# Layer 0's transposed input: read at a stride of eight floats from the tile where it lands, in place of a ScalarE copy that lays it out contiguously

## The chip, the cores and the metric

The kernel runs on one NeuronCore of a Trainium2 chip. The core has TensorE (matmul, PE in the profile, with its weight loads in a row of their own, PEld), VectorE (DVE), ScalarE (ACT), GpSimd (POOL) and SyncE (SP), which here issues every DMA. The metric is the time of one execution on the device in microseconds, and the figure given for a kernel is the median of its runs.

## The reference

Two layers of masked attention over 128 independent graphs of 128 tokens with 512 features, in float32. `x` is [128, 128, 512] and `adj` is [128, 128, 128] of booleans.

```python
# layer 0: 4 heads of 64; layer 1: 8 heads of 64, with its own layer norm ahead of the projections
def _L0_gnn_ref(x, adjacency_mask, Wq, Wk, Wv, Wo, bo):
    q, k, v = split_heads(x @ Wq), split_heads(x @ Wk), split_heads(x @ Wv)
    sim = jnp.einsum('bhid,bhjd->bhij', q, k) * scale
    sim = jnp.where(adjacency_mask[:, None, :, :], sim, neg)
    out = jnp.einsum('bhij,bhjd->bhid', softmax(sim), v)
    return merge_heads(out) @ Wo + bo

x = _layernorm(x + _L0_gnn_ref(x, adj, ...))
x = _layernorm(x + _L1_gnn_ref(x, adj, ...))   # adj or the diagonal; gamma, beta; 8 heads
```

Only one thing of it matters here: layer 0's three projections multiply `x` by weights over the feature axis. TensorE sums over the partition axis, so `x`, which arrives with tokens on the partitions, has to be turned so that features lie on the partitions and tokens along them.

## The kernel before, in words

The 128 graphs are taken in 64 groups of two (`G = 2`). A group passes through a software pipeline whose order is written out by hand: `opening`, then `step(s)` for s = 2 to 63, then `closing` and `last`. One step works on several groups at once: layer 0's projections of group s, layer 0's scores of group s - 1, its output product of group s - 2, and layer 1's stages of the groups before. Every engine runs its instructions strictly in the order in which the step emits them.

All large products are done as seven smaller ones (Strassen's scheme): a product of 2 by 2 blocks is made of seven block products of sums and differences of the blocks. "2 by 2" means here the two graphs of the group by the two halves of the features (`KH = 2` chunks of 128 features each). GpSimd makes the four sums of the input (`sums`, which calls `halves_sums`, L292). `product_0` (L362 to L399) issues layer 0's seven products; products 1, 2 and 4 take a block of the input itself, products 5, 6, 3 and 7 take one of the sums. Each product has six matmuls: query, key and value (t = 0, 1, 2) by two chunks. For query and key the input block is the moving operand, for value it is the stationary one (L384, L385). `out_product` (L402 to L427) does the same for the output projections: after each of its products VectorE adds the accumulator into the residual rows (L427), and the accumulators' banks, `a`, `c` and `f`, are used again by later products of the same seven.

The turning of `x` for groups 3 to 63 goes through memory, in five stages:

1. `turn(0, g)`: VectorE transposes blocks of 32 by 32, one instruction per graph (L219), into the tile `turned`.
2. `put`: one DMA of 512 KB writes `turned` to a scratch tensor in HBM (L204).
3. `arrive(0, g)`: four DMAs of 128 KB (L210) bring it back with the blocks on the right partitions, into `raw`, in which a partition holds 4 token blocks by 2 graphs by 4 chunks by 32 tokens. Layer 1 uses the same tile for its own input.
4. `in_order(g)`: at the start of the next step ScalarE copies `raw` into `xT0`, where the 128 tokens of a graph and chunk are contiguous; one instruction per graph (L246).
5. `sums(0, g)` on GpSimd and `product_0` on TensorE read `xT0`.

The order around these stages in a step is:

```python
        made = scores(s)
        load(s + 1)
        if s > 2:
            in_order(s)
            sums(0, s)
        masked(made, s, 0, 1, 2)
        attend(s)
```

`product_0(s, 1)` comes after `attend`; `turn(0, s + 1)` stands late in the step, among layer 1's value products and its output product (`v(s - 3, 7, 3)`, `turn(0, s + 1)`, `v(s - 3, 4)`, `out_product(1, s - 4, 6, 5)`); `arrive(0, s + 1)` is near the step's end. Groups 0, 1 and 2 are turned by TensorE itself (`transposed`), and the result is copied out of PSUM by ScalarE for one graph and by VectorE for the other (L236).

Of the kernel before, what the change touches and what calls it, by code (L numbers as in the profile page):

```python
# [10 lines left out]
F32 = mybir.dt.float32  # L11
U8 = mybir.dt.uint8
AF = mybir.ActivationFunctionType
ALU = mybir.AluOpType
# [3 lines left out]
P = 128  # L18
D = 64
G = 2  # L20
# [7 lines left out]
def kernel(ctx: ExitStack, tc: tile.TileContext, x, adj, wq, wk, wv, wo, bo,  # L28
                            gamma, beta, w_qkv, w_out, b_out, out):
    nc = tc.nc  # L30
    B, N, E = x.shape
    KC = E // P
    NG = B // G
    T = G * N
# [4 lines left out]
    one = ctx.enter_context(tc.tile_pool(name="one", bufs=1))  # L39
# [10 lines left out]
    def mm_tile(name):  # L50
        return ps_mm.tile([P, 512], F32, tag="mm", name=name)
# [102 lines left out]
    KH = KC // 2  # L154
# [42 lines left out]
    RATIO, XT, QK, V, QKV = {}, {}, {}, {}, {}  # L197
# [9 lines left out]
    def fetch(dst, scr):  # L207
        src = scr.rearrange("(a r) q x -> r q a x", r=32)
        for q in range(4):
            nc.sync.dma_start(dst[32 * q:32 * q + 32], src[:, q])  # L210

    SCR, RAW = {}, {}

    def turn(l, g):
        if not 0 <= g < NG:
            return
        t = one.tile([P, 4, G * KC * 32], F32, tag="turned", bufs=2, name=f"turned{l}_{g}")
        for b in range(G):
            nc.vector.transpose(t.rearrange("p a (b c i) -> p a b c i", b=G, c=KC)[:, :, b],  # L219
                                R[g][:, b].rearrange("p (c a i) -> p a c i", a=4, i=32))  # L220
        SCR[l] = put(t, f"scr{l}_{g}")

    def arrive(l, g):
        if not 0 <= g < NG:
            return
        RAW[l] = one.tile([P, 4, G, KC, 32], F32, tag="raw", name=f"raw{l}_{g}")
        fetch(RAW[l].rearrange("p a b c i -> p a (b c i)"), SCR[l])

    def transposed(g):

        xT = XT[0, g] = one.tile([P, KC, T], F32, tag="xT0", name=f"xT0_{g}")
        for b in range(G):
            pt = mm_tile(f"xt{g}_{b}")
            for c in range(KC):
                nc.tensor.transpose(pt[:, c * N:(c + 1) * N], R[g][:, b, c * P:(c + 1) * P], ident)
            (nc.scalar.copy, nc.vector.tensor_copy)[b](xT[:, :, b * N:(b + 1) * N],  # L236
                                                       pt.rearrange("p (c n) -> p c n", c=KC))
        sums(0, g)

    def in_order(g):  # L240

        if not 0 <= g < NG:
            return
        xT = XT[0, g] = one.tile([P, KC, T], F32, tag="xT0", name=f"xT0_{g}")
        for b in range(G):
            nc.scalar.copy(xT[:, :, b * N:(b + 1) * N].rearrange("p c (a j) -> p a c j", a=4),  # L246
                           RAW[0][:, :, b])

    def finish(g, half):

# [29 lines left out]
    def sums(l, g):  # L280
        if not 0 <= g < NG:
            return
        xs = XS[l, g] = one.tile([P, 4, KH, N], F32, tag=f"xs{l}", name=f"xs{l}_{g}")
        halves_sums(xs, XT[l, g].rearrange("p (h c) (b n) -> p b h c n", h=2, b=2))

    def halves_sums(xs, a):
        s1, s2, s3, s4 = (xs[:, i] for i in range(4))
        for o, a0, a1, op in ((s1, a[:, 1, 0], a[:, 1, 1], ALU.add),
                              (s2, s1, a[:, 0, 0], ALU.subtract),
                              (s4, a[:, 0, 1], s2, ALU.subtract),  # L290
                              (s3, a[:, 0, 0], a[:, 1, 0], ALU.subtract)):
            nc.gpsimd.tensor_tensor(o, a0, a1, op=op)  # L292


    XS, ACC, EV = {}, {}, {}
# [66 lines left out]
    def product_0(g, *which):  # L362

        if not 0 <= g < NG:
            return
        xT = XT[0, g].rearrange("p (h c) (b n) -> p b h c n", h=2, b=2)
        xs = XS[0, g]
        for i in which:
            left = {1: xT[:, 0, 0], 2: xT[:, 0, 1], 3: xs[:, 3], 4: xT[:, 1, 1], 5: xs[:, 0],
                    6: xs[:, 1], 7: xs[:, 2]}[i]  # L370
            right = {1: w0[:, :KH, 0], 2: w0[:, KH:, 0], 3: w0[:, KH:, 1], 4: ws0[:, 2],
                     5: w0[:, :KH, 1], 6: ws0[:, 0], 7: ws0[:, 1]}[i]
            bank, first = INTO[i]
            if i == 1:

                QKV[g] = two.tile([P, G, 2, 3, P], F32, tag="qkv0", name=f"qkv0_{g}")
            if first and bank == "c":
                ACC[0, bank] = mm_tile(f"c0_{g}")
            elif first:
                ACC[0, bank] = ps_st.tile([P, 512], F32, tag=f"{bank}0", name=f"{bank}0_{g}")  # L380
            acc = ACC[0, bank]
            todo = [(t, c) for t in range(3) for c in range(KH)]
            for n, (t, c) in enumerate(todo):
                lhsT, rhs = (right[:, c, t], left[:, c]) if t < 2 else (left[:, c], right[:, c, t])  # L384
                nc.tensor.matmul(acc[:, t * P:(t + 1) * P], lhsT, rhs, start=first and n == 0,  # L385
                                 stop=n == len(todo) - 1, skip_group_check=True)
            src = acc[:, :3 * P]

            def whole(b, h):
                return QKV[g][:, b, h].rearrange("p t n -> p (t n)")  # L390

            if i in (1, 5, 6):
                EV[0, i] = one.tile([P, 512], F32, tag=f"e{i}", name=f"e0_{i}_{g}")[:, :3 * P]
                nc.scalar.copy(EV[0, i], src)
            elif i == 4:
                nc.scalar.copy(whole(1, 0), src)
            else:
                b, h, e = {2: (0, 0, 1), 3: (0, 1, 6), 7: (1, 1, 5)}[i]
                nc.vector.tensor_add(whole(b, h), src, EV[0, e])  # L399
# [31 lines left out]
    SM, TOTAL, NMAX, PT, AT, SO = {}, {}, {}, {}, {}, {}  # L431
# [150 lines left out]
    def out_sums(l, g):  # L582
        if not 0 <= g < NG:
            return
        K = HEADS[l] // 2
        so = SO[l, g] = one.tile([P, 4, K // 2, N], F32, tag=("so", "xs0")[l], name=f"so{l}_{g}")
        halves_sums(so, AT[l, g].rearrange("p b (h c) n -> p b h c n", h=2))

    def addend(l, g):

# [145 lines left out]
    def step(s):  # L736

        direct = s in (2, 3)
        made = scores(s)
        load(s + 1)  # L740
        if s > 2:
            in_order(s)
            sums(0, s)
        masked(made, s, 0, 1, 2)
        attend(s)
        maxima(s, 0)
        if s > 3:
            maxima(s, 1)
        out_sums(0, s - 2)
        exps(s, 0, 0)  # L750
        product_0(s, 1)
        exps(s, 0, 1)
        out_product(0, s - 2, 1, 2, 5)
        if s == 3:
            maxima(s, 1)
        maxima(s, 2)
        product_0(s, 2)
        normalised(s, 0)
        out_product(0, s - 2, 6, 3)
        exps(s, 1, 0)  # L760
        stats(0, s - 2, 0)
        product_0(s, 6)
        exps(s, 1, 1)
        out_product(0, s - 2, 7)
        product_0(s, 5)
        out_product(0, s - 2, 4)
        stats(0, s - 2, 1)
        exps(s, 2, 0)
        product_0(s, 7)
        exps(s, 2, 1)  # L770
        normalised(s, 1)
        product_0(s, 3)
        blocks(s, 0)
        flush()
        product_0(s, 4)
        if direct:
            prepare(len(setup) - (s == 2))
        else:
            turn(1, s - 2)
        out_sums(1, s - 4)  # L780
        v(s - 3, 1, 2)
        out_product(1, s - 4, 1)
        if not direct:
            arrive(1, s - 2)
        blocks(s, 1)
        probs_arrive(s, 0)
        v(s - 3, 6, 5)
        out_product(1, s - 4, 2)
        normalised(s, 2)
        v(s - 3, 7, 3)  # L790
        turn(0, s + 1)
        v(s - 3, 4)
        flush(latest)
        cleared(s + 1, 0, 1)
        if direct:
            finish_direct(s - 2)
        else:
            finish(s - 2, 0)
        if s == 2:
            weight_sums(w1qk, wsqk, 1)  # L800
            prepare(1)
        out_product(1, s - 4, 6, 5)
        if not direct:
            finish(s - 2, 1)
        out_product(1, s - 4, 7, 3, 4)
        blocks(s, 2)
        probs_arrive(s, 1)
        stats(1, s - 4, 0)
        stats(1, s - 4, 1)
        arrive(0, s + 1)  # L810
        probs_arrive(s, 2)
        cleared(s + 1, 2)
        addend(0, s - 1)
        with_self(s - 2)
        qk(s - 2, 1, 2, 6)
        flush()
        qk(s - 2, 5)
        addend(1, s - 3)
        qk(s - 2, 7, 3, 4)
        if s == 2:  # L820
            weight_sums(w1v, wsv, 0, 1)
        if s == 3:
            weight_sums_out(1)
# [130 lines left out]
```

## Time and profile before

| | |
|---|---|
| median of three runs (lowest, highest) | 2784.31 us (2784.19, 2784.57) |
| profiled execution, from its first to its last instruction (span) | 2782.9 us |
| PE busy, of the span | 2768.0 us, 99% |
| PEld busy | 2609.2 us, 94% |
| DVE busy | 1789.9 us, 64% |
| ACT busy | 1502.5 us, 54% |
| POOL busy | 1752.2 us, 63% |
| mean granted TensorE clock | 0.999 of full |
| one step of the steady state | 42.84 us |
| L246, ScalarE's copy `xT<-raw` | 122 of 621 ns on average, 69.6 us busy |
| L219, VectorE's transpose `turned<-r` (both layers) | 242 of 678 ns |
| L292, GpSimd's sums of the inputs (both layers) | 512 of 732 to 740 ns |

The profile is of one execution of its own. For that execution the page gives the span, and no other time; the three timed runs lie 1.3 to 1.7 us above that span, which is what surrounds the instructions. A busy share says how long an engine had an instruction in work, not whether that work was on the path that sets the end; "PE" and "PEld" overlap each other by design. In the timeline a row that merges several instructions gives the start of the first and the length from there to the end of the last, so consecutive rows of PE overlap by the time that a matmul needs to drain, and the pace is read from start to start. Names are written as output <- inputs; for PE the first input is the moving operand and the second the stationary one.

### The profile page before, as it was taken

To read this page: it belongs to the slowest core of one execution; us is meant where nothing else is said; L and a number is where in the kernel's file an instruction comes from. 1 tells how busy PE (TensorE), PEld (TensorE's weight loads), DVE (VectorE), ACT (ScalarE), POOL (GpSimd) and SP (SyncE) were. 2 spreads that over 40 slices of the span, in tenths; PEclk is the share of its full clock that TensorE was granted. 3 is DMA by queue.
4 is the path that set the end of the run, shared out by engine and by line. 5 is a ranking of instruction groups with operands and counts; after the bars stand their busy time and mean duration, and the time that the engine had idled before them with its cause. 6 is when DMAs were issued, how large, how long until landed. Compare 5 with 4: busy or idle time off the path is not lost.

```text
span 2782.9 us, 63227 instructions
## 1 busy us (share of the span) xinstructions
PE 2768.0 (99%) x23317; PEld 2609.2 (94%) x23317; DVE 1789.9 (64%) x3303; ACT 1502.5 (54%) x4811; POOL 1752.2 (63%) x2311
## 2 busy tenths in 40 slices
PE   9999999999999999999999999999999999999998
PEld 8999999999999999999999999999999999999997
DVE  5766666666666666666666666666666666666665
ACT  3554555645555556455555564555555645555554
POOL 5656566666565666666656666666566666665664
PEclk9999999999999999999999999999999999999999
DMA  5345455464564554644545546455454464554532
GB/s 170 115 138 173 128 158 154 130 175 138 138 171 127 161 153 129 177 138 138 169 129 161 153 127 177 139 138 166 128 165 148 128 179 136 145 165 126 160 107 69
DMA packets 281812, 405.24 MB, mean 146 GB/s; under 512 B 44696, under 2 KB 206496, under 8 KB 281504
## 3 DMA queue, kind: packets, MB, share of 16 engines
q1 hardware_dynamic: 281504, 401.20, 49.5%
q8 instruction: 185, 3.03, 0.5%
q14 instruction: 123, 1.01, 0.1%
HBM read 205.00 MB, written 196.08 MB: 144 GB/s over the span
## 4 chain that ended last, share of the span: by engine, by line
PE 96%; issue 1%; POOL 1%; DVE 1%; DMA 1%; ACT 0%; SPq 0%; POOLq 0%; ACTq 0%; DVEq 0%
PE qka L329 16%; PE a L385 12%; PE oa L423 12%; PE qkf L329 8%; PE va L329 8%; PE av L575 6%; PE f L385 6%; PE of L423 6%; PE qkc L329 4%; PE vf L329 4%; PE c L385 3%; PE oc L423 3%; PE sc L456 2%; PE sc L462 2%; PE vc L329 2%; PE sc_a L462 2%
## 5 line engine op out<-in xcount | busy, mean ns | idle before, releaser
L514 POOL TENSOR_TENSOR sm<-sm,rec 128x1024 f32<-128x1024 f32 x192 | 364.1, 1896 | 383.4 <-DVE rec L513 383.1
L505 ACT ACTIVATE sm<-sm,nmax 128x128 f32<-128x128 f32 x1536 | 595.2, 393 | 4.9 <-DVE nmax L496 4.3
L596 POOL TENSOR_TENSOR r<-r,bias 128x1024 f32<-128x1024 f32 x128 | 302.0, 2359 | 63.5 <-ACT r L595 63.5
L427 DVE TENSOR_TENSOR r<-oa,r 128x256 f32<-128x256 f32 x508 | 212.3, 418 | 199.7 <-PE oa L423 191.6
L292 POOL TENSOR_TENSOR xs<-xT 128x256 f32<-128x256 f32 x256 | 189.4, 740 | 211.0 <-ACT xT L246 164.9
L505 ACT ACTIVATION_READ_ACCUMULATOR sm<-sm,nmax 128x1 f32 x1536 | 294.8, 192 | 0.0
L355 ACT COPY eqk<-qka 128x512 f32<-128x512 f32 x128 | 75.0, 586 | 349.3 <-PE qka L329 349.3
L490 DVE COPY_PREDICATED sm<-m,sc 128x512 f32<-128x512 uint8 x256 | 173.0, 729 | 134.9 <-PE sc L456 134.9
L329 PE MATMUL qka<-xs,wsqk 128*128 128x128 f32 x2048 | 249.7, 275 | 0.3 <-POOL xs L292 0.3
L329 PE MATMUL qkf<-xs,w 128*128 128x128 f32 x2048 | 249.8, 275 | 0.0
L529 DVE STREAM_TRANSPOSE turnedp<-sm 128x1024 f32<-128x1024 f32 x189 | 234.0, 1238 | 17.1 <-DMA scrp<-turnedp 11.8
L329 PEld LDWEIGHTS qka<-xs,wsqk 128*128 128x128 f32 x2048 | 239.0, 192 | 0.5 <-POOL xs L292 0.5
L329 PEld LDWEIGHTS qkf<-xs,w 128*128 128x128 f32 x2048 | 239.0, 192 | 0.0
L360 DVE TENSOR_TENSOR qk<-qka,eqk 128x512 f32<-128x512 f32 x64 | 44.3, 692 | 291.1 <-PE qka L329 286.1
L496 DVE TENSOR_REDUCE nmax<-sm 128x8 f32<-128x1024 f32 x192 | 226.4, 1206 | 0.1
L423 PE MATMUL oa<-wso,so 128*128 128x256 f32 x760 | 206.0, 380 | 0.7 <-DVE r L427 0.7
L423 PE MATMUL of<-wo,so 128*128 128x256 f32 x760 | 205.6, 379 | 0.7 <-POOL so L292 0.7
L615 POOL TENSOR_SCALAR ve<-mv 128x2 f32<-128x2 f32 x191 | 40.8, 214 | 261.3 <-DVE mv L608 255.1
L641 ACT ACTIVATE r<-r,shift,root 128x512 f32<-128x512 f32 x254 | 192.4, 807 | 8.7 <-POOL shift L630 4.7
L476 POOL MEMSET sm<- 128x1024 f32 x192 | 178.8, 951 | 0.0
L607 DVE BATCH_NORM_STATS2 st<-r 128x6 f32<-128x512 f32 x254 | 171.7, 676 | 4.4
L423 PEld LDWEIGHTS of<-wo,so 128*128 128x128 f32 x760 | 144.1, 190 | 20.9 <-POOL so L292 1.1
(159 smaller groups left out, 6799.9 us busy)
## 6 DMA issues: line engine op xcount, KB each, us to landing
scrp<-turnedp SPq DMA_DIRECT2D x189, 512.0 KB, 3.0
pT<-scrp SPq DMA_DIRECT2D x756, 128.0 KB, 4.1
scr<-turned SPq DMA_DIRECT2D x121, 512.0 KB, 4.4
raw<-scr SPq DMA_DIRECT2D x484, 128.0 KB, 3.6
r<-in_x_dram SPq DMA_DIRECT2D x63, 512.0 KB, 3.9
out_dram<-r SPq DMA_DIRECT2D x63, 512.0 KB, 5.0
m<-in_adj_dram SPq DMA_DIRECT2D x64, 32.0 KB, 3.7
raw_r<-in_L_gnn_w_qkv_dram SPq DMA_DIRECT2D x8, 256.0 KB, 4.2
```

Of the source, the lines that this page charges most:

```text
L292: nc.gpsimd.tensor_tensor(o, a0, a1, op=op)
L329: nc.tensor.matmul(o, lhsT, rhs, start=first and n == 0, stop=n == len(todo) - 1, skip_group_check=True)
L385: nc.tensor.matmul(acc[:, t * P:(t + 1) * P], lhsT, rhs, start=first and n == 0, stop=n == len(todo) - 1, skip_group_check=True)
L423: nc.tensor.matmul(acc, left[:, c], right[:, c], start=first and c == 0, stop=c == hk - 1, skip_group_check=True)
L427: nc.vector.tensor_add(part, acc, part)
L476: nc.gpsimd.memset(sm, NEG1 if part else NEG0)
L496: nc.vector.tensor_reduce(NMAX[part], SM[part], AX.X, ALU.max, negate=True)
L505: nc.scalar.activation(sm[:, i, k, :], sm[:, i, k, :], AF.Exp, bias=nmax[:, i, k:k + 1], accum_out=total[:, i, k:k + 1])
L514: nc.gpsimd.tensor_tensor(SM[part], SM[part], rec[:, :, :, None].to_broadcast([P, 2, K1, N]), op=ALU.mult)
L529: nc.vector.transpose(t.rearrange("p q (h r) -> p q h r", r=32), SM.pop(part).rearrange("p i k (q r) -> p q (i k) r", r=32))
L596: nc.gpsimd.tensor_tensor(R[g], R[g], (bias0, bias1)[l][:, None, :].to_broadcast([P, G, E]), op=ALU.add)
L641: nc.scalar.activation(R[g][:, b], R[g][:, b], AF.Identity, bias=shift[:, b:b + 1], scale=root[:, b:b + 1])
```

## The change

`in_order` and the tile `xT0` go. `turn(0, g)` makes VectorE write its transposes in another order, so that a partition of `raw` holds 128 tokens by 2 graphs by 4 chunks: the token is the slowest index, and the 128 tokens of one graph and chunk lie eight floats (32 bytes) apart. The DMAs move the same bytes in the same pieces. GpSimd's sums and the products 1, 2 and 4 of `product_0` read this tile directly, at the stride. Layers 0 and 1 now have raw tiles of their own, `raw0` and `raw1`; with `xT0` gone the memory used is the same. For groups 0 to 2, `transposed` copies out of PSUM into the same layout. `halves_sums` is rewritten to take its blocks from a table; for layer 1 and the output products it does what it did.

```diff
     def turn(l, g):
...
         for b in range(G):
-            nc.vector.transpose(t.rearrange("p a (b c i) -> p a b c i", b=G, c=KC)[:, :, b],
+            to = (t.rearrange("p a (b c i) -> p a b c i", b=G, c=KC)[:, :, b] if l else
+                  t.rearrange("p a (i b c) -> p b a c i", b=G, c=KC)[:, b])
+            nc.vector.transpose(to,
                                 R[g][:, b].rearrange("p (c a i) -> p a c i", a=4, i=32))
         SCR[l] = put(t, f"scr{l}_{g}")
 
     def arrive(l, g):
         if not 0 <= g < NG:
             return
-        RAW[l] = one.tile([P, 4, G, KC, 32], F32, tag="raw", name=f"raw{l}_{g}")
-        fetch(RAW[l].rearrange("p a b c i -> p a (b c i)"), SCR[l])
+        if l == 0:
+            RAW[0] = one.tile([P, N, G, KC], F32, tag="raw0", name=f"raw0_{g}")
+            fetch(RAW[0].rearrange("p (a i) b c -> p a (i b c)", a=4), SCR[0])
+        else:
+            RAW[1] = one.tile([P, 4, G, KC, 32], F32, tag="raw1", name=f"raw1_{g}")
+            fetch(RAW[1].rearrange("p a b c i -> p a (b c i)"), SCR[1])
 
     def transposed(g):
 
-        xT = XT[0, g] = one.tile([P, KC, T], F32, tag="xT0", name=f"xT0_{g}")
+        raw = RAW[0] = one.tile([P, N, G, KC], F32, tag="raw0", name=f"raw0_{g}")
...
-            (nc.scalar.copy, nc.vector.tensor_copy)[b](xT[:, :, b * N:(b + 1) * N],
+            (nc.scalar.copy, nc.vector.tensor_copy)[b](raw[:, :, b].rearrange("p n c -> p c n"),
                                                        pt.rearrange("p (c n) -> p c n", c=KC))
         sums(0, g)
-
-    def in_order(g):
-
-        if not 0 <= g < NG:
-            return
-        xT = XT[0, g] = one.tile([P, KC, T], F32, tag="xT0", name=f"xT0_{g}")
-        for b in range(G):
-            nc.scalar.copy(xT[:, :, b * N:(b + 1) * N].rearrange("p c (a j) -> p a c j", a=4),
-                           RAW[0][:, :, b])
...
     def sums(l, g):
...
-        halves_sums(xs, XT[l, g].rearrange("p (h c) (b n) -> p b h c n", h=2, b=2))
+        if l == 0:
+            halves_sums(*quarters(xs, RAW[0].rearrange("p n b (h c) -> p b h c n", h=2)))
+        else:
+            halves_sums(*quarters(xs, XT[l, g].rearrange("p (h c) (b n) -> p b h c n", h=2, b=2)))
+
+    def quarters(xs, a):
+        return [xs[:, i] for i in range(4)], {(b, h): a[:, b, h] for b in range(2) for h in range(2)}
...
     def product_0(g, *which):
...
-        xT = XT[0, g].rearrange("p (h c) (b n) -> p b h c n", h=2, b=2)
-        xs = XS[0, g]
+        xs, raw = XS[0, g], RAW[0]
         for i in which:
-            left = {1: xT[:, 0, 0], 2: xT[:, 0, 1], 3: xs[:, 3], 4: xT[:, 1, 1], 5: xs[:, 0],
-                    6: xs[:, 1], 7: xs[:, 2]}[i]
+            piece = {1: (0, 0), 2: (0, 1), 4: (1, 1)}.get(i)
+
+            def left(c):
+                return (raw[:, :, piece[0], piece[1] * KH + c] if piece else
+                        xs[:, {3: 3, 5: 0, 6: 1, 7: 2}[i], c])
+
...
-                lhsT, rhs = (right[:, c, t], left[:, c]) if t < 2 else (left[:, c], right[:, c, t])
+                lhsT, rhs = (right[:, c, t], left(c)) if t < 2 else (left(c), right[:, c, t])
...
     def step(s):
...
         if s > 2:
-            in_order(s)
             sums(0, s)
```

More of the change, by code (lines that the diff above doesn't have):

```diff
@@ L283, in sums @@
         xs = XS[l, g] = one.tile([P, 4, KH, N], F32, tag=f"xs{l}", name=f"xs{l}_{g}")
-        halves_sums(xs, XT[l, g].rearrange("p (h c) (b n) -> p b h c n", h=2, b=2))
-    def halves_sums(xs, a):
[L287 to L291, printed above, removed]
+        if l == 0:
[4 more added lines that the diff above has]
+        return [xs[:, i] for i in range(4)], {(b, h): a[:, b, h] for b in range(2) for h in range(2)}
+    def halves_sums(xs, a):
+        s1, s2, s3, s4 = xs
+        for o, a0, a1, op in ((s1, a[1, 0], a[1, 1], ALU.add),
+                              (s2, s1, a[0, 0], ALU.subtract),
+                              (s4, a[0, 1], s2, ALU.subtract),
+                              (s3, a[0, 0], a[1, 0], ALU.subtract)):
             nc.gpsimd.tensor_tensor(o, a0, a1, op=op)
@@ L586, in out_sums @@
         so = SO[l, g] = one.tile([P, 4, K // 2, N], F32, tag=("so", "xs0")[l], name=f"so{l}_{g}")
-        halves_sums(so, AT[l, g].rearrange("p b (h c) n -> p b h c n", h=2))
+        halves_sums(*quarters(so, AT[l, g].rearrange("p b (h c) n -> p b h c n", h=2)))
     def addend(l, g):
```

## The prediction

> **What bounds the kernel now.** I read four views, in this order. First the page's busy times and its chain of waits, then one whole step of the steady state by engine, for 1352.51 to 1395.35 us:
>
> ```profile
> PE 2768.0 (99%) x23317; PEld 2609.2 (94%) x23317; DVE 1789.9 (64%) x3303; ACT 1502.5 (54%) x4811; POOL 1752.2 (63%) x2311
> PE 96%; issue 1%; POOL 1%; DVE 1%; DMA 1%; ACT 0%; SPq 0%; POOLq 0%; ACTq 0%; DVEq 0%
> 1352.51:1395.35 42.84, 42.84 (x365) 40.47 (x366) 27.68 (x52) 23.38 (x75) 27.30 (x37) 1.00 0.49 149
> ```
>
> The reader is to see that TensorE has no gap: 42.84 us of matmul in a 42.84 us step, and a chain that is 96% PE. ScalarE, from which the change takes work, is busy 23.4 us of 42.8 and has 0% of the chain. So the edit is worth what it does to PE, and what it makes late for PE.
>
> Third, the timeline, PE alone, where layer 0's products begin:
>
> ```profile
> 1355.21 1.16 PE L385 MATMUL a<-xT,w 128*128 128x128 f32 x8
> 1356.21 0.61 PE L385 MATMUL a<-w,xT 128*128 128x128 f32 x4
> ...
> 1357.95 1.05 PE L385 MATMUL c<-xT,w 128*128 128x128 f32 x8
> 1358.85 0.61 PE L385 MATMUL c<-w,xT 128*128 128x128 f32 x4
> 1359.29 0.60 PE L423 MATMUL oa<-wso,so 128*128 128x256 f32 x2
> ```
>
> Columns: start, length, then output <- moving operand, stationary operand. One matmul of the loop leaves two records, so a product's six are twelve passes: eight with xT moving (query and key), four with xT stationary (value). Start to start, 8 passes take 1358.85 - 1357.95 = 0.90 us and 4 take 0.44, so a pass costs 111.5 ns for 128 columns, 0.87 ns a column. The weight loads run beside the matmuls at the same pace, one per pass (40.47 us of 42.84).
>
> Fourth, who waits for the ScalarE copy that goes, and what ScalarE does after it (waits; timeline, ACT):
>
> ```profile
> POOL xs L292 <- ACT xT L246: 164.9, 61, 5.5
> 1350.15 1.14 ACT L246 COPY xT<-raw 128x512 f32<-128x512 f32 x2
> 1353.59 0.59 ACT L578 COPY aT<-av 128x512 f32<-128x512 f32 x1 [2.29 <-PE av L575]
> ```
>
> GpSimd alone waits for it, in time in which it had nothing else; behind it ScalarE sits idle 2.29 us until PE delivers. Nothing that PE waits for comes earlier when the copy goes.
>
> [...]
>
> **The change part by part.**
>
> *Removed:* L246, 122 copies of 621 ns, 1.24 us a step on ScalarE. Off the path, as shown: worth 0. A gain would need a PE wait that ends earlier, and I see none.
>
> *PE reads layer 0's input at the stride.* Products 1, 2 and 4 are touched; 3, 5, 6 and 7 read the sums, which stay contiguous. [...] I take half rate[...]: 128 columns cost 128 x 0.83 = 107 ns more (0.83: 215 ns for 256 columns in L423, four passes in 0.86 us). [...] Both operands have the stride in some passes: eight stream it; four load it as weights, and a load that takes 214 ns no longer fits under a 111.5 ns matmul. The first of the four is loaded under the last slow stream, so 8 + 3 = 11 slow passes: 11 x 107 = 1.18 us a product, 3.53 us a step, and for 64 groups **+226 us**. Nothing covers it, PE being full.
>
> *VectorE writes the transposes at the stride* (L219 for layer 0, two a step). Where they stand (timelines, DVE and PE):
>
> ```profile
> 1332.33 1.29 DVE L219 STREAM_TRANSPOSE turned<-r 128x512 f32<-128x512 f32 x2
> 1333.72 0.42 DVE L427 TENSOR_TENSOR r<-oa,r 128x256 f32<-128x256 f32 x1
> 1334.58 0.42 DVE L427 TENSOR_TENSOR r<-of,r 128x256 f32<-128x256 f32 x1 [0.44 <-PE of L423]
> ...
> 1332.65 1.03 PE L423 MATMUL oa<-wso,so 128*128 128x256 f32 x4
> 1333.52 1.03 PE L423 MATMUL of<-wo,so 128*128 128x256 f32 x4
> 1334.38 1.03 PE L423 MATMUL oa<-wso,so 128*128 128x256 f32 x4
> ```
>
> Behind them in VectorE's queue is the evacuation of layer 1's output product 6, and PE may not write that bank again (product 7, its weights loaded from 1334.26) before VectorE has read it (done 1334.14). Slack: 0.10 us between the transposes' end (1333.62) and the evacuation, 0.12 after it, together 0.22. [...] A pair is then 1.1 us late, PE waits 0.88 us in each of the 59 steps that have this product (s = 4 to 62): **+52 us** (0 to 75). It can't be caught up, since PE has no idle time later.
>
> *GpSimd's four sums* (735 ns; 128 more columns cost 272 ns) read the stride. [...] They can start at 1348.72, when the bias addition ends, instead of 1351.37: 2.65 us earlier. PE's first need behind them is layer 0's output sum s1, ready at 1354.84, its product's weights loaded at 1357.31: another 2.47 us. So 0, up to 5.1 us a step (2.7 times the duration); past that product 5 is late.
>
> *Queues.* SP's DMAs stay in number, size and order (one put of 512 KB, four fetches of 128 KB). The put waits for VectorE and slips 1.1 us: issued at 1334.22, landed 4.4 us later, so 2.9 us before the first fetch at 1341.53: covered, and with it the fetches of probabilities queued behind. The fetch now waits until PE and GpSimd have read the tile instead of ScalarE: product 4 is over at 1367.7, the next fetch comes at 1384.4, 16.7 us later. POOL issues no DMA. Two raw tiles instead of one only loosen.
>
> *The opening's three direct groups:* ScalarE and VectorE write at the stride once for each[...]; only the first stands in PE's way: +1 us (0 to 4).
>
> **Sum:** 226 + 52 + 1 = 279 us. Against the profiled execution's span of 2782.9 that is 3062; the runs' median lies 1.4 us above that span, so **3063 us** (+10%).
>
> **The rivals.**
>
> 1. *Only VectorE pays* (0.20). [...] 2784 + 53 = 2837 (2800 to 2865).
> 2. *One of TensorE's operands pays* (0.12): weights alone 4 x 107 x 192 products = 82 us, streams alone 164; with the transposes 2919 or 3001 (2870 to 3010).
> 3. *More than half rate* (0.09): [...] (above 3120).
> 4. *Not slower* (0.06; and 0.01 for over 0.2% faster). One place decides, PE at L385: if its ports hold 0.87 ns a column, and the transposes stay under 0.11 us longer each, both fit into today's slack and nothing is left but a copy that cost nothing: 2784 (2779 to 2789). For it, GpSimd's and the queues' cover[...]. That the change does not do what it says I rule out: the copy's instruction is gone and the operands' steps are written in the diff.
>
> **How the numbers follow.** My forecast, both TensorE operands and the transposes, has 0.52, with its own range of 2995 to 3120 (PE 190 to 250, VectorE 20 to 77). The time is that of this case. The 8-in-10 range runs over cases 1, 2 and this, 2795 to 3120: 0.84 less their tails. A measurement can tell 0.2%, 5.6 us. Slower: 0.52 + 0.20 + 0.12 + 0.09 = 0.93; within: 0.06; faster: 0.01.
>
> **What would show it.** In the changed profile: matmuls of L385 that stream the raw tile start 215 to 220 ns apart, as do those that load it, and products of the sums stay at 111.5; if the former stay at 111.5 too, the main step is wrong. L219 for layer 0 takes 1.0 to 1.4 us, for layer 1 still 0.67, and PE gains a wait for VectorE's L427 of some 0.9 us a step; without it the 52 us fall. ScalarE's busy time falls by about 70 us. GpSimd's sums from the raw tile near 1 us, ahead of need; a PE wait for xs or so would break that step.

## The result, and the profile after

| | before | changed |
|---|---|---|
| median | 2784.44 us (2784.19 to 2785.08) | **3061.32 us** (3060.71 to 3061.97) |
| ratio to before, 95% interval | | **1.0994** (1.0979 to 1.1010) |
| span of the profiled execution | 2782.9 us | 3059.3 us |
| one step of the steady state | 42.84 us | 47.27 us |

Before's median is of four executions here, one more than above. The kernel is 277 us, 10%, slower. A step grew by 4.43 us. The page of the changed kernel, busy times and chain of waits; then one of its steps by engine:

```profile
PE 3032.3 (99%) x23317; PEld 2830.4 (93%) x23317; DVE 1824.8 (60%) x3303; ACT 1455.4 (48%) x4689; POOL 1790.0 (59%) x2311
PE 93%; DVE 5%; issue 1%; POOL 0%; ACT 0%; DMA 0%; SPq 0%; POOLq 0%; ACTq 0%; DVEq 0%
```

```profile
976.37:1023.64 47.27, 47.04 (x363) 43.94 (x363) 28.20 (x52) 22.68 (x73) 27.87 (x36) 1.00 0.47 135
```

PE issues the same 23317 matmuls, is still busy for 99% of the span at full clock (1.00 in this step), and yet needs 264 us more for them. That is the sign to look for: not a wait, but the same instructions taking longer. The one new thing on the chain is VectorE, 5%. The timeline of PE, from product 2 of layer 0 on (bank `c`), shows which instructions grew:

```profile
980.35 2.02 PE L391 MATMUL c<-raw,w 128*128 128x128 f32 x8
982.19 0.99 PE L391 MATMUL c<-w,raw 128*128 128x128 f32 x4
983.02 0.60 PE L429 MATMUL oa<-wso,so 128*128 128x256 f32 x2
...
983.88 1.05 PE L391 MATMUL a<-xs,ws 128*128 128x128 f32 x8
984.78 0.61 PE L391 MATMUL a<-ws,xs 128*128 128x128 f32 x4
985.22 0.60 PE L429 MATMUL oa<-wso,so 128*128 128x256 f32 x2
```

Start to start, eight passes that stream the raw tile take 1.84 us, 230 ns each; four that load it as weights take 0.83 us, 207 ns each; the product of the sums beside them still takes 0.90 and 0.44 us, 112 and 110 ns a pass. Product 2 grew from 1.34 to 2.67 us.

Next the place where the transposes stand. An evacuation is VectorE's addition of a product's accumulator into the residual rows (L433, L427 before); it frees the accumulator's bank. The timeline of VectorE, then that of PE, and last what PE waited for (waits, PE alone):

```profile
1000.22 2.04 DVE L221 STREAM_TRANSPOSE turned<-r 128x512 f32<-128x512 f32 x2
1002.10 0.41 DVE L433 TENSOR_TENSOR r<-oa,r 128x256 f32<-128x256 f32 x1
1002.47 0.42 DVE L433 TENSOR_TENSOR r<-of,r 128x256 f32<-128x256 f32 x1
```

```profile
1000.54 1.03 PE L429 MATMUL oa<-wso,so 128*128 128x256 f32 x4
1001.40 1.03 PE L429 MATMUL of<-wo,so 128*128 128x256 f32 x4
1002.66 1.10 PE L429 MATMUL oa<-wso,so 128*128 128x256 f32 x4 [0.23 <-DVE r L433]
1003.59 1.03 PE L429 MATMUL of<-wo,so 128*128 128x256 f32 x4
```

```profile
PE oa L429 <- DVE r L433: 13.4, 59, 0.3
```

The row of before that follows the three of PE in the prediction:

```profile
1335.24 1.03 PE L423 MATMUL of<-wo,so 128*128 128x256 f32 x4
```

The four PE rows of each kernel are products 6, 5, 7 and 3 of the output product. Two transposes take 2.04 us instead of 1.29. The evacuation of product 6 starts at 1002.10 without a wait, 1.56 us after product 6 itself (1000.54); before it was 1.07 us (1332.65 to 1333.72), so it is 0.49 us late. Product 7 starts 1.26 us after product 5, where it was 0.86, and product 3 another 0.93 us later, where it was 0.86: from product 5 to product 3 it is 2.19 us against 1.72, and PE loses 0.47 us. The waits view books less, 0.23, because the row of product 5 runs to 1002.43, 0.17 us beyond its pace of 0.86, and covers the first part of the gap. It happens 59 times, once in each step that has this product: 59 x 0.47 = 28 us.

GpSimd, the one that had waited for the copy (timeline, POOL):

```profile
969.76 0.66 POOL L295 TENSOR_TENSOR xs<-raw 128x256 f32<-128x256 f32 x1
...
972.24 1.14 POOL L295 TENSOR_TENSOR xs<-raw 128x256 f32<-128x256 f32 x1
```

The sums are done at 973.4, ten microseconds before the first product that reads them (983.88).

### The profile page after: what moved, and what is told of

It reads as the page before. It is cut to its first block, busy times and chain, and to the rows that moved or that the text cites. A ratio compares the mean times of both kernels' runs of the same rounds, so it can differ in the third digit from the quotient of the medians.

```text
span 3059.3 us, 63048 instructions
## 1 busy us (share of the span) xinstructions
PE 3032.3 (99%) x23317; PEld 2830.4 (93%) x23317; DVE 1824.8 (60%) x3303; ACT 1455.4 (48%) x4689; POOL 1790.0 (59%) x2311
## 4 chain that ended last, share of the span: by engine, by line
PE 93%; DVE 5%; issue 1%; POOL 0%; ACT 0%; DMA 0%; SPq 0%; POOLq 0%; ACTq 0%; DVEq 0%
PE a L391 17%; PE qka L332 15%; PE oa L429 9%; PE qkf L332 7%; PE av L581 6%; PE c L391 6%; PE f L391 6%; PE va L332 6%; DVE turned L221 4%; PE qkc L332 4%; PE of L429 4%; PE vf L332 4%; PE oc L429 3%; PE sc L462 2%; PE sc L468 2%; PE vc L332 2%
## 5 line engine op out<-in xcount | busy, mean ns | idle before, releaser
L433 DVE TENSOR_TENSOR r<-oa,r 128x256 f32<-128x256 f32 x508 | 211.4, 416 | 309.9 <-PE oa L429 298.8
L295 POOL TENSOR_TENSOR so<-aT 128x128 f32<-128x128 f32 (+1 forms) x254 | 150.5, 593 | 135.5 <-ACT aT L584 129.1
L221 DVE STREAM_TRANSPOSE turned<-r 128x512 f32<-128x512 f32 x242 | 200.1, 886 | 0.0
```

The costliest lines, as they stand in the source:

```text
L221: nc.vector.transpose(to, R[g][:, b].rearrange("p (c a i) -> p a c i", a=4, i=32))
L433: nc.vector.tensor_add(part, acc, part)
```

## The experiments

The theory after the result: both operands of TensorE, the moving one that is streamed and the stationary one that is loaded as weights, and VectorE's writes pay for the stride, and the costs add. (The expectations below call TensorE's ways to its two operands its ports.) The rivals: only one operand pays; the costs depend on each other; the cost grows with the distance between the words, so that half the stride would cost less and pieces further apart more.

### e1 to e3: the operands one at a time

All three start from the changed kernel and put a contiguous copy behind the raw tile, so that the layout of memory, VectorE's writes and GpSimd's reads stay those of the change; they differ in what TensorE reads. The two layers share one raw tile again to make room, and the opening makes a second copy of each graph out of PSUM.

```diff
+    def in_order(g):
...
+            nc.scalar.copy(xT[:, :, b * N:(b + 1) * N], RAW[0][:, :, b].rearrange("p n c -> p c n"))
...
-            def left(c):
-                return (raw[:, :, piece[0], piece[1] * KH + c] if piece else
-                        xs[:, {3: 3, 5: 0, 6: 1, 7: 2}[i], c])
+            def left(c, t):
+                if piece and (CONDITION):        # e1: False   e2: t < 2   e3: t == 2
+                    return raw[:, :, piece[0], piece[1] * KH + c]
+                if piece:
+                    return XT[0, g][:, piece[1] * KH + c, piece[0] * N:(piece[0] + 1) * N]
+                return xs[:, {3: 3, 5: 0, 6: 1, 7: 2}[i], c]
```

> The changed kernel with ScalarE's copy put back behind it: VectorE still writes its transposes at the stride and GpSimd's sums still read it, but TensorE reads a contiguous copy. Theory (TensorE's strided reads and VectorE's strided writes each pay, and the costs add): what is left is VectorE's 0.40 us of stall in 59 steps, 24 us over the kernel before, so 2805 to 2815 us, with passes of 111.5 ns and a transpose of 1.09 us. Rival (the costs are not separate: [...]the stall for VectorE is there only because TensorE runs late): under 2790 or over 2830.

> As e1, but the query and key matmuls stream the strided tile, while the value matmuls load their weights from the contiguous copy. Theory: eight passes of 230 ns in each of three products, 8 x 118 ns x 192 = 181 us, and VectorE's 24: about 2990 us. Rival (only one of TensorE's two ports minds the stride, here the weights'): about 2810. Rival (a product is slow as a whole once either operand is strided): near 3060.

> The other half: value matmuls load strided weights, query and key stream the contiguous copy. Theory: four loads of about 207 ns a product, 4 x 97 ns x 192 = 74 us, and VectorE's 24: about 2883 us; together with e2 the excess over the kernel before, VectorE's part counted once, makes the whole 277. If the first strided load could hide under the pass ahead of it, as the prediction had it, it is only three: 2864. Rival (streams alone pay): about 2810.

| | TensorE reads at the stride | median | ratio to before (95%) | above e1, per product |
|---|---|---|---|---|
| e1 | nothing | 2817.98 us | 1.0122 (1.0107 to 1.0137) | |
| e2 | streams | 2995.82 us | 1.0761 (1.0743 to 1.0779) | 178 us / 192 = 0.93 us |
| e3 | weights | 2910.83 us | 1.0455 (1.0439 to 1.0470) | 93 us / 192 = 0.48 us |
| changed | both | 3061.32 us | 1.0994 (1.0979 to 1.1010) | (243 + 7) us / 192 = 1.30 us |

The 192 are products 1, 2 and 4 of 64 groups. The 7 us are what e1 to e3 lose in the opening, as shown below, where the changed kernel has no second copies; e4 less before gives the same 250 us without e1.

The timelines of PE for product 2, first e2, then e3:

```profile
451.81 2.02 PE L405 MATMUL c<-raw,w 128*128 128x128 f32 x8
453.65 0.63 PE L405 MATMUL c<-w,xT 128*128 128x128 f32 x4
454.11 0.60 PE L443 MATMUL oa<-wso,so 128*128 128x256 f32 x2
```

```profile
438.60 1.05 PE L405 MATMUL c<-xT,w 128*128 128x128 f32 x8
439.49 1.11 PE L405 MATMUL c<-w,raw 128*128 128x128 f32 x4
440.44 0.60 PE L443 MATMUL oa<-wso,so 128*128 128x256 f32 x2
```

In e2 the eight streams take 1.84 us and the four passes with contiguous weights 0.46; in e3 the streams take 0.89 us and the four strided loads 0.95, 237 ns each. So each operand pays by itself, and about the same: over the whole time 0.93 us / 8 = 116 ns a stream and 0.48 us / 4 = 121 ns a load, in these rows 230 - 112 = 118 and 237 - 110 = 127. Together they would make 1.41 us; both at once cost 1.30. In the rows of product 2 it is 0.96 + 0.50 = 1.46 against 2.67 - 1.34 = 1.33. The missing 0.11 to 0.13 us is about one load: where slow streams go ahead, the first strided load runs under the last of them (0.83 us for the four in the changed kernel, 0.95 in e3). Both one-operand rivals fall, and so does that of a product slow as a whole. e3 came out at 2911 us where 2883 was expected: that sum took 97 ns a load from the changed kernel, where one of the four is covered, and left out the 7 us of the opening. e2's 2996 is over its 2990 by about these 7 us.

e1 ended 34 us above before, where 21 to 31 were expected. Its step is 43.29 us (290.33 - 247.04 between the same rows of its chain), 0.45 above before; 59 x 0.45 = 27 us. The other 7 us lie in the opening: product 2 of the sixth group starts at 158.46 us before and at 165.89 in e1, 7.4 us later. e6 and e7, which like e1 make second copies there, start it 4.3 and 3.4 us late, and e8, which makes none, 1.0. So these copies are the likely cause; no run changes them alone.

### e4: the two transposes apart

```diff
-        v(s - 3, 7, 3)
-        turn(0, s + 1)
+        v(s - 3, 7)
+        turn(0, s + 1, 0)
+        v(s - 3, 3)
+        turn(0, s + 1, 1)
         v(s - 3, 4)
```

> The changed kernel with its two strided transposes apart: the first is emitted between layer 1's value products 7 and 3, the second where it was. Nothing else differs. Theory (TensorE waits 0.40 us a step because both stand in one piece ahead of the evacuation of output product 6): the second ends before that evacuation is due, the wait of TensorE for L433 goes, and the kernel is 20 to 26 us faster than the changed one, 3035 to 3042 us. Rival (the wait only moves to the evacuation of value product 3, or is made up elsewhere): 3055 to 3062.

Measured: 3033.86 us, 27.5 us faster than the changed kernel and 1 us under the range expected, which counted 0.40 us a step where PE loses 0.47; ratio to before 1.0899 (1.0883 to 1.0915). The timeline of VectorE in e4:

```profile
429.36 1.10 DVE L226 STREAM_TRANSPOSE turned<-r 128x512 f32<-128x512 f32 x1
430.31 0.41 DVE L369 TENSOR_TENSOR v<-vf,ev 128x256 f32<-128x256 f32 x1
430.64 1.08 DVE L226 STREAM_TRANSPOSE turned<-r 128x512 f32<-128x512 f32 x1
431.57 0.40 DVE L439 TENSOR_TENSOR r<-oa,r 128x256 f32<-128x256 f32 x1
432.41 0.42 DVE L439 TENSOR_TENSOR r<-of,r 128x256 f32<-128x256 f32 x1 [0.43 <-PE of L435]
```

The transposes are as slow as without this edit, 1.08 to 1.10 us. The evacuation of value product 3 (`v<-vf`) still comes 1.56 us after its product starts, where it was 1.07, but PE does not wait for that bank. The evacuation of output product 6 comes 0.84 us ahead of that of product 5, as before (0.86), and PE's 59 waits are gone from its waits. This is the same 27 us that e1 shows in its step, reached from the other side: the VectorE part is a stall by position, not a cost of the slow instruction as such. What is left over before, 250 us, is TensorE: e4's step is 46.81 us, 3.97 above before, and three products that grew by 1.33 us each make 3.99.

### e5 to e7: which spacing costs

These keep e2's arrangement (streams from the raw tile, weights from the copy) and change only how tokens lie in it, with the reads by GpSimd and ScalarE to match. Each run has one of the three new lines. In e5 and e6, runs of 32 tokens go at a stride of four and of two floats, half and a quarter of e2's spacing; in e7, pairs of adjacent tokens stand 64 bytes apart, so that every word has a neighbour while the pieces are further apart than e2's. The DMAs are those of the change.

```diff
-                  t.rearrange("p a (i b c) -> p b a c i", b=G, c=KC)[:, b])
+                  t.rearrange("p a (b i k) -> p b a k i", b=G, k=4)[:, b])               # e5
+                  t.rearrange("p a (b m i k) -> p b a m k i", b=G, m=2, k=2)[:, b])      # e6
+                  t.rearrange("p a (i b c w) -> p b a c i w", b=G, c=KC, w=2)[:, b])     # e7
```

> As e2 (query and key stream the tile where it lands, value's weights come from ScalarE's contiguous copy), but with tokens four floats (16 bytes) apart, in runs of 32 tokens. [...] Theory[...]: as e2, 2990 to 3000 us, 230 ns a streamed pass, transposes near 1.08 us. Rival[...]: close to e1's 2818 us.

> The same with tokens two floats (8 bytes) apart[...]. Theory[...]: passes of 111.5 ns, and only what e1 loses to VectorE: 2810 to 2820 us. Rival (pairs of adjacent words decide for TensorE[...]): 230 ns a pass and 2990 to 3000 us. For VectorE's writes the pair rule expects 1.08 us a transpose here too[...].

> The same with pairs of tokens adjacent (8 bytes), the pairs 64 bytes apart: [...] VectorE then writes runs of two, 0.67 us a transpose, and the kernel is near the one before, 2785 to 2795 us (the opening has two more copies a graph). Rival (the distance between the pieces costs[...]): streamed passes clearly above 112 ns and more than 2850 us.

| | spacing | nearest word of the same walk | streamed pass | median | ratio (95%) |
|---|---|---|---|---|---|
| e2 | 32 bytes | 32 bytes | 230 ns | 2995.82 us | 1.0761 (1.0743 to 1.0779) |
| e5 | 16 bytes | 16 bytes | 226 ns | 2992.60 us | 1.0749 (1.0733 to 1.0765) |
| e6 | 8 bytes | 8 bytes | 114 ns | 2790.29 us | 1.0022 (1.0014 to 1.0030) |
| e7 | pairs, 64 bytes apart | 4 bytes, adjacent | 112 ns | 2786.88 us | 1.0010 (1.0001 to 1.0018) |

The timeline of PE, product 2, in e5, and the same rows in e6 and e7:

```profile
1006.29 1.99 PE L410 MATMUL c<-raw,w 128*128 128x128 f32 x8
1008.10 0.62 PE L410 MATMUL c<-w,xT 128*128 128x128 f32 x4
```

```profile
1021.03 1.07 PE L410 MATMUL c<-raw,w 128*128 128x128 f32 x8
1021.94 0.60 PE L410 MATMUL c<-w,xT 128*128 128x128 f32 x4
```

```profile
1019.22 1.05 PE L407 MATMUL c<-raw,w 128*128 128x128 f32 x8
1020.12 0.61 PE L407 MATMUL c<-w,xT 128*128 128x128 f32 x4
```

And the transposes of both layers (instructions of one line: shortest, median, longest ns), in e2 and then in e6:

```profile
L221 DVE STREAM_TRANSPOSE turned<-r x242: 668/1086/1121, 64.1 to 2865.8; 128x512 f32<-128x512 f32 x121
```

```profile
L221 DVE STREAM_TRANSPOSE turned<-r x242: 668/670/714, 57.9 to 2661.9; 128x512 f32<-128x512 f32 x121
```

Half of these 242 transposes are layer 1's, contiguous in every run, so e2's median is only the edge of the slow half: layer 0's take 1.08 to 1.12 us in e2 and up to 1.16 in e5.

At 16 and at 32 bytes a streamed pass takes double (226 and 230 ns); at 8 bytes it takes 114 ns and in pairs 64 bytes apart 112, next to nothing above the 111.5 before. VectorE's writes are slow and fast in the same layouts: in e6 and e7 the 242 transposes, layer 0's among them, take 668 to 715 ns. So e5's rival, a time close to e1's, falls with 2992.60 us, and e7's with 112 ns. The pair rule falls too: in e6 no two words in a row are adjacent, and neither engine slows by more than 3% (114 against 111.5 ns, 670 against 670). What the four layouts show is no more than this: in both free ones the word before or after lies within 8 bytes, in both slow ones it is 16 bytes away or more. What makes the difference in the hardware, and where between 8 and 16 bytes it begins, they do not show; a stride of three floats was not run. e6 missed its whole-time figure, 2810 to 2820, because that still counted VectorE's stall, which is gone: PE waits for an evacuation once, 0.7 us, and the time is 27.7 us below e1's. e7 stayed in its range.

### e8: the whole change at 8 bytes

e5 to e7 left the weights contiguous. In e8 all 128 tokens of a graph and chunk lie in one run, two floats apart, and streams and weights are both read from it, with no copy by ScalarE. The excerpt leaves out the sixteen fetches and the two reordered calls that the expectation names.

```diff
-                  t.rearrange("p a (i b c) -> p b a c i", b=G, c=KC)[:, b])
+                  t.rearrange("p a (b m i k) -> p b a m k i", b=G, i=32, k=2)[:, b])
...
-            RAW[0] = one.tile([P, N, G, KC], F32, tag="raw0", name=f"raw0_{g}")
-            fetch(RAW[0].rearrange("p (a i) b c -> p a (i b c)", a=4), SCR[0])
+            RAW[0] = one.tile([P, G, 2, N, 2], F32, tag="raw0", name=f"raw0_{g}")
+            fetch(RAW[0].rearrange("p b m (a i) k -> p a (b m) (i k)", a=4), SCR[0])
```

> What the change set out to do[...]: no copy by ScalarE, and all of layer 0's products, weights too, read the tile where it lands, tokens two floats (8 bytes) apart over all 128. For that layout the return from memory takes sixteen DMAs of 32 KB a group in place of four of 128 KB, issued after the last fetch of probabilities, and GpSimd makes the output sums of layer 0 before the input sums. Theory[...]: passes of 111.5 ns in streams and in weight loads, transposes of 0.67 us, 2780 to 2790 us, the time of the kernel before. Rival (the weights' port needs its words adjacent): loads of about 207 ns, 60 to 95 us more, 2845 to 2880 us. Rival (the tile lands too late behind twelve more DMA issues): TensorE waits for the raw tile's DMA or for the sums, and passes keep 111.5 ns.

Measured: 2791.84 us, ratio 1.0024 (1.0015 to 1.0034). The timeline of PE:

```profile
1018.50 1.07 PE L398 MATMUL c<-raw,w 128*128 128x128 f32 x8
1019.41 0.63 PE L398 MATMUL c<-w,raw 128*128 128x128 f32 x4
1019.87 0.60 PE L436 MATMUL oa<-wso,so 128*128 128x256 f32 x2
```

Streams take 114 ns a pass and loads 115, against 111.5 and 110 before. So loads, like streams, cost little more at 8 bytes than contiguous ones, and the rival with slow loads falls. So does the rival of the late tile: no wait of PE for the raw tile's DMA shows among its waits. The copy is gone and the time is that of before within 7 us, 2 us more than was expected; the few nanoseconds a pass are most of it (8 x 2.5 + 4 x 5 = 40 ns a product, 8 us in 192). It gains nothing either: what it frees is ScalarE, and PE was never waiting for it. No version here beats the kernel before.

## Why the prediction was right, point by point

- **The bound, and the removed copy worth nothing: right.** PE stayed at 99%, and e8, which has no copy either and whose passes take 114 and 115 ns, is not faster than before (1.0024).
- **TensorE at half rate: right in kind, 24 us too small.** 226 us were forecast; with VectorE's stall out of the way, e4 less before, it was 250. The count of 11 slow passes a product was right: e2 and e3 apart cost about one load more than both together. The mis-sized term is the pass: 107 ns more were taken, and 118 (250 us / 192 / 11) were measured. The 107 doubled only the slope of 0.84 ns a column (0.215 us / 256; the prediction writes 0.83), while a streamed pass doubled as a whole, from 111.5 to 230 ns. That a strided pass takes double was the author's estimate: no operand of the kernel before has such a stride, so no trace of it could show this.
- **VectorE's transposes: right in place, twice too large.** 52 us were forecast and 27 measured, in 59 steps as foretold. The mis-sized term is the price of a transpose. Its length grew by about 0.42 us (from 0.67 to between 1.08 and 1.10), and what delays the next instruction grew by less still, because a row's length includes a tail in which the next instruction already runs. From start to start a contiguous transpose takes 0.62 us (1.29 for the pair less 0.67 for the second) and a strided one 0.94 (1000.22 to 1002.10 for two). So the pair holds VectorE up by some 0.64 us, not 1.1. The slack was nearer to its 0.22: the evacuation came 0.49 us late, so 0.15 us was covered ahead of it, and PE lost 0.47 of that, so 0.02 behind it, where 0.12 had been taken. The 1.1 us was the author's estimate: no trace of the kernel before has a transpose that writes at this stride.
- **The sum: 3063 against 3061.3 us, closer than its terms by luck.** One term was 24 us short and the other 25 us long. The forecast was good to some 25 us, not to 2. Its 1 us for the opening was not measured apart.
- **The rivals.** The first, VectorE alone, and the second, one operand alone, fall with e2 and e3; the third, a pass of far more than twice the time, and the fourth, nothing slower, fall with the 230 ns of a streamed pass. The size of the third was the author's estimate, with no trace behind it.
- **GpSimd and the queues: right where it counts.** The sums of layer 0 take 0.88 us on average, 0.14 over the contiguous ones, where near 1 us was forecast, and they end long before need. No DMA wait became one of PE's: of DMAs it waits once, 3.4 us for the first load of `x`, as before.
- **ScalarE's busy time: wrong, and without effect.** It fell by 47 us (1502.5 to 1455.4), not by the copies' 70. No other instruction of it grew to make up for that: added up from the two traces, their durations are 75 us less, and the 122 copies alone are 76. What shrank is the time in which rows overlap, which busy time counts once; why was not looked into.

## What to carry to other kernels

Before an engine is made to read a tile "where it lands", see how far apart the words lie in a walk along the innermost axis. In float32 here, words 8 bytes apart cost at most 5 ns a pass of TensorE (114 ns a streamed pass, 115 a load, against 111.5 and 110), while at 32 bytes a pass took 230 ns streamed and 237 loaded, and VectorE's transpose took 1.6 times as long (1.08 us against 0.67). ScalarE's copy, for which only GpSimd waited, cost nothing (e8, without it, takes 2791.84 us, no less than before), while the slow operands of PE, which bounds the kernel, cost all of their added time, 250 us. The slower transposes on VectorE cost PE only what exceeded the slack behind them (0.47 of 0.64 us a step), and in e4 moving one instruction past another brought that back (27.5 us).

## What the runs showed of the hardware that was not expected

- The moving and the stationary operand of TensorE pay for words 32 bytes apart about alike: 118 and 127 ns more a pass of 128 columns (product 2 of e2 and e3).
- Words at 8 bytes cost 2.5 to 5 ns a pass, next to nothing, though no two are adjacent (e6, e8; 114 and 115 ns).
- VectorE's transpose wrote at 8 bytes in 670 ns, as contiguous (e6), and at 16 or 32 bytes in 1.08 us and more (e5, e2).
- A transpose's row outlasts the start of the next instruction: two strided ones, of 1.08 to 1.10 us each, let it start after 1.88 us. Slack read from row ends is wrong by such tails.
- ScalarE's copy out of the raw tile took 1154 ns at 32 bytes, 641 from pairs and 621 from runs of 32 (e2, e7, before), so its reads nearly double as well.
